# Layer 2's expert FFN in a fused four-layer kernel: features dealt out every eleventh, SiLU formed from tanh, and another order of units

## The chip, the cores and the metric

One core of a Trainium2 chip runs the whole program in one launch. The metric is device time in microseconds (us) from launch to end; lower is better. The engines that appear in the text: TensorE (PE in the profile; PEld is its weight loading, which overlaps it), VectorE (DVE), ScalarE (ACT), GpSimd (POOL) and SyncE (SP, which here only issues transfers). SBUF is the on-chip memory of 128 partitions, PSUM the memory that TensorE writes its results to.

## The reference

The reference is a gated network of four layers over x, 64 sequences of 64 tokens with 128 features (4096 tokens). Each layer adds a mixer and an FFN to x, each behind a layer norm and a scalar gate tanh(g):

```python
x = x + tanh(g_xattn[n]) * mixer_n(layernorm(x), ctx)
x = x + tanh(g_ffn[n]) * ffn_n(layernorm(x))          # n = 0..3, eight stages in all
```

The change is in layer 2's FFN, a mixture of 8 experts with 176 features each, of which every token uses the best two, plus one shared expert of 176 features:

```python
E, K, I = (8, 2, 176)
probs = jax.nn.softmax(x @ gate_w.T, axis=-1)
topk_w, topk_i = jax.lax.top_k(probs, K)
topk_w = topk_w / jnp.sum(topk_w, axis=-1, keepdims=True)
combine = jnp.sum(jax.nn.one_hot(topk_i, E) * topk_w[..., None], axis=1)
g = jnp.einsum('th,ehi->eti', x, w_gate)
u = jnp.einsum('th,ehi->eti', x, w_up)
eo = jnp.einsum('eti,eih->eth', jax.nn.silu(g) * u, w_down)
out = jnp.einsum('te,eth->th', combine, eo)
sg = jax.nn.sigmoid(x @ shared_gate_w.T)
out = out + sg * (jax.nn.silu(x @ sw_gate) * (x @ sw_up) @ sw_down)
```

The other stages that the text names: layer 0's FFN (a mixture with one expert chosen per head; lines 1236 and 1291 are its large products), layer 1's attention (lines 1349 to 1474), layer 1's FFN (an autoencoder picks an adapter per sequence; line 1585 gathers its rows), layers 2's and 3's attention (function `attend8`, lines 1637 to 1728), and layer 3's FFN, which quantises by the largest value over all tokens and therefore can't finish before every token has come through.

## The kernel before

**Units.** The 4096 tokens are eight groups of 512. A stage n applied to a group g is a unit, written "ng". The list `ORDER` (line 2135) names all 64 units in the order in which they are recorded; a group passes through its stages in turn, and groups overlap. The first unit of a stage also records the stage's constants, and the weights of a stage are loaded after the first unit of the stage before.

**The planner.** Nothing is issued as written. Every call on an engine is recorded as an operation with its inputs, outputs and an estimated duration (`cost`, line 221). `Plan.order` (line 401) then schedules all operations at once: at each step it picks, among the operations that are ready, the one that can start first, preferring earlier recorded ones, and so fixes the order of instructions on every engine and queue. On the chip every engine works through its fixed list in that order. Temporary tiles come from pools of slots (`SLOTS`, line 41: 45 slots of 2 KB per partition, `b2k`, and the 8 banks of PSUM, `ps`). `TABLES` (line 218) says which function of ScalarE needs which table; where an operation needs another table than the last one, the planner adds 1300 ns to it, and holds it back for up to 1000 ns in favour of others. `Tanh` is marked as needing no table of its own. Where the planner sees TensorE without work, `keep_clock` (line 482) puts in fillers: products of the identity with itself whose result nobody reads. They are recorded under line 2158.

**Layer 2's FFN (lines 1816 to 1926).** Per group of 512 tokens:

- `ln_T`: layer norm and transposition, so that xT has features on partitions and tokens along the row.
- `route` (1847): scores, softmax, best two experts and their weights, and the shared expert's sigmoid, which ends as cw, nine combine weights per token (gate factor included).
- `spread` (1885): cw is transposed (1889), copied (1891) and written to device memory as cwd, nine rows of 512 (1893).
- The nine experts' features lie side by side as 9 x 176 = 1584 columns. They are taken in 13 chunks: twelve of 128 columns and one of 48. A chunk has features on partitions. Since 176 is no multiple of 128, a chunk holds parts of one or two experts, and each chunk has its own tile cb, in which every partition holds its expert's combine weights for the 512 tokens. cb is filled from cwd by one or two transfers (1906), 20 per unit, 160 in all.
- Per chunk: two products on TensorE, pg (1914) and pu (1915); SiLU of pg on ScalarE (1917); times pu on VectorE (1918); times cb on GpSimd (1919); and the down product on TensorE, summed over the chunks in one bank (1920). For the chunk of 48, one product with both weights side by side (1911).
- At the end a copy (1922), a transposition back and an addition to x (1924).

The weights stand in SBUF for the whole run: gate and up weights as 128 x 1536, loaded in one transfer each (1824) on ScalarE's queue; the down weights as 13 chunks of 128 rows, loaded by 29 transfers (1833) on SyncE's queue.

Of the kernel before, what the change touches and what calls it, by code (L numbers as in the profile page):

```python
# [23 lines left out]
AF = mybir.ActivationFunctionType  # L24
ALU = mybir.AluOpType
AX = mybir.AxisListType

P = 128
# [5 lines left out]
GT = 512  # L34
# [730 lines left out]
def bc(ap, axis, n):  # L765

    ap = ap.unsqueeze(axis)
    shape = list(ap.shape)
    shape[axis] = n
    return ap.to_broadcast(shape)  # L770
# [8 lines left out]
def first_onehot(k, vals, best, rank, tag):  # L779

    nc = k.nc
    p, m, n = vals.shape
    eq = k.tile([p, m, n], tag=tag + "e")
    nc.vector.tensor_tensor(eq, vals, bc(best, 2, n), ALU.is_equal)
    nc.vector.tensor_tensor(eq, eq, bc(rank, 1, m), ALU.mult)
    top = k.tile([p, m], tag=tag + "t")
    nc.vector.tensor_reduce(top, eq, AX.X, ALU.max)
    oh = k.tile([p, m, n], tag=tag + "o")  # L790
    nc.vector.tensor_tensor(oh, eq, bc(top, 2, n), ALU.is_equal)
    return oh
# [42 lines left out]
def transpose4(k, src):  # L835

    ps = k.ps()
    k.plan.wait(src)
    for t in range(4):
        k.nc.tensor.transpose(ps[:, t * P : (t + 1) * P], src[:, t, :], k.ident)  # L840
    return ps


def ln_T(k, g):

    ps = transpose4(k, layernorm(k, g))
    xT = k.tile([P, GT], tag="xT")
    k.nc.scalar.copy(xT, ps)
    return xT
# [966 lines left out]
def l2_ffn_weights(k):  # L1816
    k.l2f = {"gate": k.load("l2f_gate")}

    last = k.l2f["last"] = k.fixed("w_l2f_last", [P, 112])
    k.nc.gpsimd.memset(last, 0.0)  # L1820
    at, end = k.done
    for n, name in enumerate(("wg", "wu")):
        t = k.l2f[name] = k.fixed("w_l2f_" + name, [P, 1536])
        k.nc.scalar.dma_start(out=t, in_=k.a["l2f_" + name][:, :1536])
        k.nc.scalar.dma_start(out=last[:, 64 * n : 64 * n + 48], in_=k.a["l2f_" + name][:, 1536:])
        k.plan.after = k.plan.ops[at + (end - at) * (n + 1) // 3]
    src = k.a["l2f_wd"]
    wd = k.l2f["wd"] = k.fixed("w_l2f_wd", [P, 13, P])
    for n in range(18):
        r = 88 * n  # L1830
        while r < 88 * n + 88:
            end = min(88 * n + 88, (r // P + 1) * P)
            k.nc.sync.dma_start(
                out=wd[r % P : r % P + end - r, r // P, :], in_=src[r - 88 * n : end - 88 * n, n * P : (n + 1) * P]
            )
            r = end


def l2_ffn(k):
    nc = k.nc  # L1840
    E, I, HID = 8, 176, 9 * 176
    CH = [(c, min(P, HID - c)) for c in range(0, HID, P)]
    W = k.l2f

    gate = k.tg[:, 1, 2:3]

    def route(xT, g):

        pr = k.ps()
        for t in range(TG):  # L1850
            nc.tensor.matmul(
                pr[:, t * (E + 1) : (t + 1) * (E + 1)], xT[:, t * P : (t + 1) * P], W["gate"], start=True, stop=True
            )
        lg = pr[:, : TG * (E + 1)].rearrange("p (t e) -> p t e", e=E + 1)
        pb = k.tile([P, TG, E], tag="pb")
        m = k.tile([P, 4, TG], tag="m")
        nc.vector.tensor_reduce(m[:, 0], lg[:, :, 0:E], AX.X, ALU.max)
        nc.vector.tensor_tensor(pb, lg[:, :, 0:E], bc(m[:, 0], 2, E), ALU.subtract)
        nc.scalar.activation(pb, pb, AF.Exp)
        nc.vector.tensor_reduce(m[:, 1], pb, AX.X, ALU.add)  # L1860
        nc.vector.reciprocal(m[:, 1], m[:, 1])
        nc.vector.tensor_tensor(pb, pb, bc(m[:, 1], 2, E), ALU.mult)
        nc.vector.tensor_reduce(m[:, 2], pb, AX.X, ALU.max)
        oh1 = first_onehot(k, pb, m[:, 2], k.rank8, tag="l2oh1")
        nc.vector.scalar_tensor_tensor(pb, oh1, -2.0, pb, ALU.mult, ALU.add)
        nc.vector.tensor_reduce(m[:, 3], pb, AX.X, ALU.max)
        oh2 = first_onehot(k, pb, m[:, 3], k.rank8, tag="l2oh2")

        nc.vector.tensor_tensor(m[:, 0], m[:, 2], m[:, 3], ALU.add)
        nc.vector.reciprocal(m[:, 0], m[:, 0])  # L1870
        nc.vector.scalar_tensor_tensor(m[:, 2], m[:, 2], gate, m[:, 0], ALU.mult, ALU.mult)
        nc.vector.scalar_tensor_tensor(m[:, 3], m[:, 3], gate, m[:, 0], ALU.mult, ALU.mult)
        cw = k.tile([P, TG, E + 1], tag="cw")
        nc.vector.tensor_tensor(oh1, oh1, bc(m[:, 2], 2, E), ALU.mult)
        nc.vector.tensor_tensor(oh2, oh2, bc(m[:, 3], 2, E), ALU.mult)
        nc.vector.tensor_tensor(cw[:, :, 0:E], oh1, oh2, ALU.add)

        sg = k.tile([P, TG], tag="sg1")
        nc.scalar.activation(sg, lg[:, :, E], AF.Exp, scale=-1.0)
        nc.vector.tensor_scalar(sg, sg, 1.0, None, ALU.add)  # L1880
        nc.vector.reciprocal(sg, sg)
        nc.vector.tensor_scalar(cw[:, :, E], sg, gate, None, ALU.mult)
        return cw

    def spread(cw):

        pc = k.ps()
        for t in range(TG):
            nc.tensor.transpose(pc[: E + 1, t * P : (t + 1) * P], cw[:, t, :], k.ident)
        cT = k.tile([E + 1, GT], tag="cwT")  # L1890
        nc.scalar.copy(cT, pc[: E + 1, :])
        d = k.dram([E + 1, GT], "cwd")
        nc.sync.dma_start(out=d, in_=cT)
        return d

    def unit(g):
        xT = ln_T(k, g)
        cwd = spread(route(xT, g))
        py = k.ps()
        for c, (c0, cn) in enumerate(CH):  # L1900
            cb = k.tile([P, GT], tag="cb")
            r = c0
            while r < c0 + cn:
                e = r // I
                end = min(c0 + cn, (e + 1) * I)
                nc.sync.dma_start(out=cb[r - c0 : end - c0, :], in_=cwd[e : e + 1, :].to_broadcast([end - r, GT]))
                r = end
            pg = k.ps()
            if cn < P:
                pu = pg[64 : 64 + cn]  # L1910
                nc.tensor.matmul(pg[: 64 + cn], W["last"], xT, start=True, stop=True)
            else:
                pu = k.ps()
                nc.tensor.matmul(pg, W["wg"][:, c0 : c0 + cn], xT, start=True, stop=True)  # L1914
                nc.tensor.matmul(pu, W["wu"][:, c0 : c0 + cn], xT, start=True, stop=True)  # L1915
            h = k.tile([P, GT], tag="h")
            nc.scalar.activation(h[:cn], pg[:cn], AF.Silu)  # L1917
            nc.vector.tensor_tensor(h[:cn], h[:cn], pu, ALU.mult)  # L1918
            nc.gpsimd.tensor_tensor(h[:cn], h[:cn], cb[:cn], ALU.mult)  # L1919
            nc.tensor.matmul(py, W["wd"][:cn, c, :], h[:cn], start=(c == 0), stop=(c == len(CH) - 1))  # L1920
        yT = k.tile([P, TG, P], tag="yT")
        nc.scalar.copy(yT.rearrange("p t i -> p (t i)"), py)
        xg = k.x[g].rearrange("p t d -> p (t d)")
        nc.vector.tensor_tensor(xg, xg, transpose4(k, yT), ALU.add)

    return unit
# [44 lines left out]
def l3_ffn(k):  # L1971
# [163 lines left out]
ORDER = [  # L2135
    (int(n), int(g))
    for n, g in (
        "02 00 03 01 06 04 10 05 11 20 07 21 30 31 40 12 41 50 13 51 16 22 14 60 15 61 23 70 26 32 17 24 "
        "71 42 25 33 36 27 43 34 46 52 35 44 62 45 37 53 56 47 63 54 66 55 64 65 72 57 67 73 76 74 75 77"
    ).split()  # L2140
]

# [1 line left out]
def program(tc, a):  # L2144
    with ExitStack() as es:
# [9 lines left out]
        for g in early:  # L2155
            nc.sync.dma_start(out=k.x[g], in_=xin[g])
        constants(k)
        plan.spare = (sys._getframe().f_lineno, k.ident, k.ident.t.writes[-1][0])
        mixers = (l0_xattn, l0_ffn, l1_xattn, l1_ffn, l2_xattn, l2_ffn, l3_xattn)
        weights = (None, l0_ffn_weights, l1_xattn_weights, l1_ffn_weights, l2_xattn_weights, l2_ffn_weights,  # L2160
                   l3_xattn_weights)
        layers = [None] * 8
# [123 lines left out]
```

## Time and profile before

| | us |
|---|---|
| median of 18 runs | 1902.12 |
| lowest and highest of them | 1893.21, 1907.34 |
| the profiled execution | 1899.2 |
| its span, first to last instruction | 1897.5 |
| mean granted TensorE clock in it | 0.973 |

| engine | busy us | share of the span | instructions |
|---|---|---|---|
| PE | 1812.7 | 96% | 16703 |
| PEld | 1066.6 | 56% | 16703 |
| DVE | 1361.0 | 72% | 3194 |
| ACT | 1106.5 | 58% | 2957 |
| POOL | 1024.1 | 54% | 1655 |

One fp32 product on TensorE appears in the profile as two instructions (two passes), each with a weight load; so 104 products are 208 rows. The ends of matrix products are modelled, so that a pass of 512 columns has a duration of 592 ns in the rows though the next may start earlier. In a row of the groups, the number after the bar is the group's busy time, then the mean duration of one in ns, then the time in which the engine stood idle just before members of the group, and what ended most of that. In the chain of waits, the work that ended last is followed back from the end, step by step, to what released it: PE has 70% of it, DVE 11%, POOL 8%, ACT 4%. 121.11 MB move by DMA in 122231 packets, a mean of 64 GB/s.

### The profile page before, as it was taken

To read this page: it belongs to the slowest core of one execution; us is meant where nothing else is said; L and a number is where in the kernel's file an instruction comes from. 1 tells how busy PE (TensorE), PEld (TensorE's weight loads), DVE (VectorE), ACT (ScalarE), POOL (GpSimd) and SP (SyncE) were. 2 spreads that over 40 slices of the span, in tenths; PEclk is the share of its full clock that TensorE was granted. 3 is DMA by queue.
4 is the path that set the end of the run, shared out by engine and by line. 5 is a ranking of instruction groups with operands and counts; after the bars stand their busy time and mean duration, and the time that the engine had idled before them with its cause. 6 is when DMAs were issued, how large, how long until landed. Compare 5 with 4: busy or idle time off the path is not lost.

```text
span 1897.5 us, 44773 instructions
## 1 busy us (share of the span) xinstructions
PE 1812.7 (96%) x16703; PEld 1066.6 (56%) x16703; DVE 1361.0 (72%) x3194; ACT 1106.5 (58%) x2957; POOL 1024.1 (54%) x1655
## 2 busy tenths in 40 slices
PE   7999999999999999999999999999899989999996
PEld 4555456655554445645465655675466555555675
DVE  6786887679858476667877578769458966855667
ACT  6664347745463345524368543887367766867655
POOL 7862446645433454303548354837477469476546
PEclk8899999999999999999999999999799989999999
DMA  6302230013325221031300021000141034153021
GB/s 191 113 22 82 57 101 20 2 39 115 98 76 147 60 72 46 15 103 36 95 21 13 20 65 59 24 2 3 38 115 33 29 97 120 30 141 101 32 74 45
DMA packets 122231, 121.11 MB, mean 64 GB/s; under 512 B 58378, under 2 KB 78485, under 8 KB 122013
## 3 DMA queue, kind: packets, MB, share of 16 engines
q1 hardware_dynamic: 112541, 102.66, 19.1%
q10 hardware_dynamic: 6400, 9.25, 1.6%
q0 software_dynamic: 3072, 6.33, 1.2%
q8 instruction: 132, 2.16, 0.5%
q14 instruction: 86, 0.70, 0.1%
HBM read 98.22 MB, written 8.18 MB: 56 GB/s over the span
## 4 chain that ended last, share of the span: by engine, by line
PE 70%; DVE 11%; POOL 8%; ACT 4%; issue 3%; DMA 3%; SPq 0%; another core or an unknown queue 0%; ACTq 0%; DVEq 0%; POOLq 0%
PE ps L1236 11%; PE ps L1291 8%; PE ps L840 8%; POOL b L776 5%; PE ps L1920 4%; PE ps L1914 4%; PE ps L1915 4%; PE ps L1470 3%; PE ps L1701 3%; PE ps L1349 3%; PE ps L1457 2%; PE ps L1560 2%; PE ps L1263 2%; PE ps L1663 2%; DVE b2k L1289 2%
## 5 line engine op out<-in xcount | busy, mean ns | idle before, releaser
L776 POOL TENSOR_TENSOR b<-b,neghalf 128x8 f32<-128x8 f32 (+1 forms) x208 | 303.3, 1458 | 17.0
L1291 PE MATMUL ps<-b2k,w_l0f_oe 128*128 128x512 f32 x512 | 233.2, 599 | 4.5 <-DMA b2k<-ohd 1.9
L1236 PE MATMUL ps<-w_l0f_ve,b2k 128*128 128x512 f32 x512 | 236.2, 602 | 0.5 <-DVE b4k L1105 0.2
L775 POOL TENSOR_SCALAR b<-b 128x8 f32<-128x8 f32 (+1 forms) x208 | 44.2, 213 | 320.4 <-DVE b L804 197.2
L1289 DVE TENSOR_TENSOR b2k<-b2k,b2k 128x512 f32<-128x512 f32 x256 | 174.2, 728 | 29.3 <-PE ps L1291 11.4
L1242 DVE COPY_PREDICATED b2k<-b1k,ps 128x512 f32<-128x512 int32 x224 | 161.8, 726 | 44.0 <-PE ps L1236 26.2
L1919 POOL TENSOR_TENSOR b2k<-b2k,b2k 128x512 f32<-128x512 f32 (+1 forms) x104 | 130.8, 1284 | 109.6 <-DMA b2k<-cwd 60.9
L1104 DVE TENSOR_REDUCE b<-ps 128x8 f32<-128x512 f32 x224 | 146.4, 681 | 52.0 <-PE ps L1674 14.8
L1291 PEld LDWEIGHTS ps<-b2k,w_l0f_oe 128*128 128x128 f32 x512 | 93.3, 190 | 121.2 <-issue 78.1
L1107 ACT ACTIVATE b4k<-b4k 128x64 f32<-128x64 f32 x512 | 125.8, 250 | 46.3 <-DVE b4k L1105 44.1
L1105 DVE TENSOR_TENSOR b4k<-ps,b 128x512 f32<-128x512 f32 x224 | 148.7, 678 | 4.0 <-PE ps L840 2.2
L1236 PEld LDWEIGHTS ps<-w_l0f_ve,b2k 128*128 128x128 f32 x512 | 93.5, 191 | 102.3 <-issue 84.1
L840 PE MATMUL ps<-ident,b2k 128*128 128x128 f32 x896 | 133.4, 277 | 9.1 <-ACT b2k L815 3.0
L840 PEld LDWEIGHTS ps<-ident,b2k 128*128 128x128 f32 x896 | 102.5, 141 | 67.2 <-issue 33.9
L840 PE MATMUL ps<-ident,b4k 128*128 128x128 f32 x896 | 127.3, 278 | 5.9 <-ACT b4k L1689 1.6
L840 PEld LDWEIGHTS ps<-ident,b4k 128*128 128x128 f32 x896 | 102.5, 142 | 50.4 <-issue 28.6
L1918 DVE TENSOR_TENSOR b2k<-b2k,ps 128x512 f32<-128x512 f32 (+1 forms) x104 | 70.0, 682 | 75.9 <-ACT b2k L1917 38.5
L1360 DVE TENSOR_TENSOR b2k<-ps,b 128x512 f32<-128x512 f32 x128 | 87.4, 686 | 30.4 <-POOL b L1357 18.4
L1689 ACT ACTIVATE b4k<-b4k 128x512 f32<-128x512 f32 x128 | 76.1, 630 | 51.0 <-DVE b4k L1105 45.0
L1354 DVE TENSOR_REDUCE b<-b2k 128x8 f32<-128x512 f32 x128 | 84.7, 677 | 27.6 <-ACT b2k L1351 24.8
L1920 PE MATMUL ps<-b2k,w_l2f_wd 128*128 128x512 f32 (+1 forms) x208 | 102.3, 610 | 2.0 <-POOL b2k L1919 1.9
L1440 POOL TENSOR_TENSOR b4k<-b4k,b 128x512 f32<-128x512 f32 x64 | 67.5, 1075 | 65.9 <-DVE b L1437 54.9
(368 smaller groups left out, 4091.3 us busy)
## 6 DMA issues: line engine op xcount, KB each, us to landing
b2k<-ohd SPq DMA_DIRECT2D x256, 128.0 KB
b2k<-cwd SPq DMA_DIRECT2D x40, 256.0 KB
b2k<-in_ctxT SPq DMA_DIRECT2D x32, 256.0 KB
b2k<-b2k SPq DMA_DIRECT2D x128, 64.0 KB
b2k<-b2k SPq DMA_DIRECT2D x32, 128.0 KB
b2k<-cwd SPq DMA_DIRECT2D x16, 224.0 KB
b2k<-cwd SPq DMA_DIRECT2D x16, 192.0 KB
b2k<-cwd SPq DMA_DIRECT2D x16, 160.0 KB
```

The source lines that it names most:

```text
L776: k.nc.gpsimd.tensor_tensor(out, out, k.neghalf[:, :n], ALU.pow)
L840: k.nc.tensor.transpose(ps[:, t * P : (t + 1) * P], src[:, t, :], k.ident)
L1104: nc.vector.tensor_reduce(mx, src, AX.X, ALU.max)
L1105: nc.vector.tensor_tensor(out, src, bc(mx, 2, S), ALU.subtract)
L1107: nc.scalar.activation(out[:, n, :], out[:, n, :], AF.Exp, accum_out=den[n])
L1236: nc.tensor.matmul(pe, xT[:, t * P : (t + 1) * P], W["ve"][:, e * 512 : (e + 1) * 512], start=True, stop=True)
L1242: nc.vector.copy_predicated(acc, bc(ohi[:, t * H : (t + 1) * H, e], 2, DH), pe.rearrange("p (h d) -> p h d", d=DH))
L1289: nc.vector.tensor_tensor(so, oT[c], pick[:, u, :], ALU.mult)
L1291: nc.tensor.matmul(py, W["oe"][:, n * P : (n + 1) * P], so, start=(n == 0), stop=(n == C * E - 1))
L1360: nc.vector.tensor_tensor(n.rearrange("p c (r d) -> p (c r) d", r=2), ps.rearrange("p (h d) -> p h d", d=DH), bc(r, 2, DH), ALU.mult)
L1919: nc.gpsimd.tensor_tensor(h[:cn], h[:cn], cb[:cn], ALU.mult)
L1920: nc.tensor.matmul(py, W["wd"][:cn, c, :], h[:cn], start=(c == 0), stop=(c == len(CH) - 1))
```

## The change

1. **Features every eleventh.** The 8 x 176 = 1408 features of the eight experts are 128 x 11. Chunk c (0 to 10) now holds on partition q the feature 11 q + c, read from the weights with a step of 11 columns. The expert of that feature is (11 q + c) // 176 = q // 16 for every c. So one tile cbe holds the combine weights for all eleven chunks, and one tile cbs, with the shared expert's weight on every partition, serves the two chunks of the shared expert (128 and 48 features, as columns 1408 to 1583). Two transfers per unit fill them. The down weights are loaded so that their rows follow the same order, by 16 transfers of 8 x 11 rows and three for the shared expert.
2. **SiLU from tanh.** silu(g) = g (1 + tanh(g / 2)) / 2. ScalarE computes t = tanh(pg / 2); VectorE computes w = pg times cb and then h = (t + 1) times pu; GpSimd multiplies h by w. The factor 1/2 goes into the combine weights when they are copied after their transposition (1890 of the changed kernel).
3. **Order of units.** The list ORDER has the same 64 units in another order; the first group that enters layer 1's attention, whose keys are prepared early, is group 1 where it was group 0.

Line numbers inside `l2_ffn` move by -1 or by a few lines: 1911, 1912 and 1908 are the changed kernel's products for gate, up and the last chunk, 1915 the tanh, 1917 and 1918 VectorE's products, 1919 GpSimd's, 1920 the down product.

```diff
@@ l2_ffn_weights
     for n, name in enumerate(("wg", "wu")):
-        t = k.l2f[name] = k.fixed("w_l2f_" + name, [P, 1536])
+        t = k.fixed("w_l2f_" + name, [P, 1536])
         k.nc.scalar.dma_start(out=t, in_=k.a["l2f_" + name][:, :1536])
+        k.l2f[name] = [t[:, c:1408:11] for c in range(11)] + [t[:, 1408:]]
...
-    for n in range(18):
-        r = 88 * n
-        while r < 88 * n + 88:
-            end = min(88 * n + 88, (r // P + 1) * P)
-            k.nc.sync.dma_start(
-                out=wd[r % P : r % P + end - r, r // P, :], in_=src[r - 88 * n : end - 88 * n, n * P : (n + 1) * P]
-            )
-            r = end
+    for n in range(16):
+        k.nc.sync.dma_start(
+            out=wd[8 * n : 8 * n + 8, 0:11, :], in_=src[:, n * P : (n + 1) * P].rearrange("(q c) d -> q c d", c=11)
+        )
+    for p0, c, n, r0, rows in ((0, 11, 16, 0, 88), (88, 11, 17, 0, 40), (0, 12, 17, 40, 48)):
+        k.nc.sync.dma_start(out=wd[p0 : p0 + rows, c, :], in_=src[r0 : r0 + rows, n * P : (n + 1) * P])
@@ l2_ffn, spread
-        nc.scalar.copy(cT, pc[: E + 1, :])
+        nc.scalar.activation(cT, pc[: E + 1, :], AF.Copy, scale=0.5)
@@ l2_ffn, unit
         cwd = spread(route(xT, g))
+        cbe = k.tile([P, GT], tag="cbe")
+        nc.sync.dma_start(out=cbe, in_=cwd[0:E, :].unsqueeze(1).to_broadcast([E, 16, GT]))
+        cbs = k.tile([P, GT], tag="cbs")
+        nc.sync.dma_start(out=cbs, in_=cwd[E : E + 1, :].to_broadcast([P, GT]))
         py = k.ps()
         for c, (c0, cn) in enumerate(CH):
-            cb = k.tile([P, GT], tag="cb")
-            r = c0
-            while r < c0 + cn:
-                e = r // I
-                end = min(c0 + cn, (e + 1) * I)
-                nc.sync.dma_start(out=cb[r - c0 : end - c0, :], in_=cwd[e : e + 1, :].to_broadcast([end - r, GT]))
-                r = end
+            cb = cbe if c < 11 else cbs
...
-                nc.tensor.matmul(pg, W["wg"][:, c0 : c0 + cn], xT, start=True, stop=True)
-                nc.tensor.matmul(pu, W["wu"][:, c0 : c0 + cn], xT, start=True, stop=True)
+                nc.tensor.matmul(pg, W["wg"][c], xT, start=True, stop=True)
+                nc.tensor.matmul(pu, W["wu"][c], xT, start=True, stop=True)
             h = k.tile([P, GT], tag="h")
-            nc.scalar.activation(h[:cn], pg[:cn], AF.Silu)
-            nc.vector.tensor_tensor(h[:cn], h[:cn], pu, ALU.mult)
-            nc.gpsimd.tensor_tensor(h[:cn], h[:cn], cb[:cn], ALU.mult)
+            nc.scalar.activation(h[:cn], pg[:cn], AF.Tanh, scale=0.5)
+            w = k.tile([P, GT], tag="hw")
+            nc.vector.tensor_tensor(w[:cn], pg[:cn], cb[:cn], ALU.mult)
+            nc.vector.scalar_tensor_tensor(h[:cn], h[:cn], 1.0, pu, ALU.add, ALU.mult)
+            nc.gpsimd.tensor_tensor(h[:cn], h[:cn], w[:cn], ALU.mult)
@@ ORDER
-        "02 00 03 01 06 04 10 05 11 20 07 21 30 31 40 12 41 50 13 51 16 22 14 60 15 61 23 70 26 32 17 24 "
-        "71 42 25 33 36 27 43 34 46 52 35 44 62 45 37 53 56 47 63 54 66 55 64 65 72 57 67 73 76 74 75 77"
+        "01 03 02 00 11 04 10 21 05 20 31 13 06 12 30 41 07 14 40 51 15 23 22 50 61 16 24 60 33 32 71 17 "
+        "25 43 42 70 34 26 44 35 53 52 27 45 36 54 46 37 55 63 62 47 56 64 57 65 66 73 72 67 74 75 76 77"
```

## The prediction

> **What bounds the kernel now.** I read the page's slices first, then the groups of instructions, the stretches, TensorE's own waits, and timelines around single instructions. The slices show busy tenths in 40 equal parts of the span.
>
> ```profile
> PE   7999999999999999999999999999899989999996
> DVE  6786887679858476667877578769458966855667
> ACT  6664347745463345524368543887367766867655
> ```
>
> TensorE (PE) is at nine tenths nearly everywhere; the others have room. A busy PE is not a PE at its peak, so I looked for proof: in the chain of waits 54 passes of L1291 follow each other in 23.18 us, 0.43 us for a 512-column pass, and wherever layer 2's FFN runs its passes also start 0.43 us apart. PE is the bound, and a change elsewhere pays only through PE's gaps: visible idle time, and the fillers (L2158) that the planner puts where it sees a gap. The groups (line, engine, operation, tiles, count, busy us, mean ns, idle before):
>
> ```profile
> L1917 ACT ACT_TABLE_LOAD x41 | 52.6, 1283 | 1.8 <-PE ps L1701 0.9 <-PE ps L1914 0.3
> L1689 ACT ACT_TABLE_LOAD x31 | 39.8, 1283 | 2.9 <-DVE b4k L1105 2.4
> L1918 DVE TENSOR_TENSOR b2k<-b2k,ps 128x512 f32<-128x512 f32 x96 | 64.5, 682 | 72.1 <-ACT b2k L1917 35.0 <-PE ps L1915 29.7 <-ACT b2k L1114 6.5
> L1563 DVE SCALAR_TENSOR_TENSOR b2k<-ps,w_l1f_bd,b2k 128x512 f32<-128x512 f32 x64 | 43.3, 743 | 7.4 <-PE ps L1560 7.4
> L2158 PE MATMUL ps<-ident 128*128 128x128 f32 x494 | 66.7, 286 | 1.4 <-POOL ident L859 1.4
> ```
>
> The reader sees 72 table loads between SiLU and Exp, the price of an instruction of the kind added on VectorE (743 ns), and 66.7 us of fillers. Six of the eight FFN units of layer 2 run between 1350 and 1800 us. The stretches (length; busy us of PE, PEld, DVE, ACT, POOL; clock):
>
> ```profile
> 1350.00:1800.00 450.00, 435.02 (x3942) 263.06 (x3941) 311.23 (x885) 315.63 (x574) 281.69 (x530) 0.97 0.27 74
> ...
> 1450.00:1500.00 50.00, 49.05 (x365) 26.53 (x362) 45.40 (x108) 36.61 (x68) 22.20 (x49) 1.00 0.12 35
> ```
>
> PE idles 450 - 435.0 = 15.0 us there. What ended that idle time (us in total, times, longest):
>
> ```profile
> PE ps L1604 <- DVE b4k L1105: 2.9, 1, 2.9
> PE ps L1920 <- POOL b2k L1919: 1.9, 2, 1.3
> ...
> PE ps L840 <- DVE b2k L1918: 1.6, 1, 1.6
> ...
> PE ps L840 <- ACT b4k L1689: 1.1, 2, 0.7
> PE ps L1701 <- ACT b2k L1693: 0.9, 2, 0.7
> ```
>
> So the edited lines and the ScalarE lines beside them hold PE up for only 1.9 + 1.6 + 1.1 + 0.9 = 5.5 us.
>
> **The change, part by part.**
>
> *Fillers and order.* The built programs' instruction lists hold the same 9350 matrix products and transposes on PE in both kernels; only their order and the fillers differ, 247 before and 214 after. Up to the first L0 units there are 46 against 51; from there on 201 against 163. The missing ones are those that stood between layer 2's and layer 3's units (15 and some 30); the chain at the end, where the quantisation needs a maximum over all tokens, keeps its fillers. One costs 66.7 / 247 = 0.270 us, so 33 fewer are -8.9 us. Bounds: 0, if the planner's gaps merely open again as waits, and -8.9. I take -8.9, because the one list is closed over exactly the stretches in which the other had holes.
>
> *SiLU to tanh.* ScalarE's Activate stays one per chunk (104, about 598 ns, L1917). The lists hold 94 table loads before and 14 after: 80 x 1.283 = 102.6 us of ScalarE work go. ScalarE is 70% busy in the late stretch (315.6 of 450), so most of this is off the path; what PE has waited for it is the 1.1 + 0.9 us above, and through L1918, which stood 35.0 us behind L1917, another 1.6, all within the 5.5. Around one switch (start, us, instruction):
>
> ```profile
> 1378.22 0.60 ACT L1917 ACTIVATE b2k<-ps 128x512 f32<-128x512 f32 x1
> 1378.84 1.28 ACT L1107 ACT_TABLE_LOAD   x1
> 1380.13 0.26 ACT L1107 ACTIVATE b4k<-b4k 128x64 f32<-128x64 f32 x1
> ```
>
> The load begins 0.02 us after one Activate and ends 0.01 us ahead of the next. The Trainium skill ("ScalarE: Activation LUTs", What ACT_TABLE_LOAD costs) adds a drain of about 1.38 us, 2.66 us per switch, which would free an estimated 213 us; this trace shows no such drain. As PE's waits behind ScalarE are measured by themselves, the sum stays the same by either.
>
> *The products.* VectorE did one product per chunk (682 ns) and now does two: the gate times the combine weight, again PSUM with SBUF (682 ns), and (tanh + 1) times up, of L1563's kind: 104 x 0.743 = +77.3 us on VectorE. GpSimd's product stays (104 x about 1284 ns, L1919). In the late stretch, 78 of the 104 chunks of before, VectorE goes from 311.2 to 369.2 of 450 us, 82%. What hides it: PE's own queue, as at 1450 to 1500 us, where VectorE is 91% busy (45.4 of 50) and PE still 98%. Without that cover each chunk would cost 0.743 us. I take 0; bounds 0 and +23 us (third rival below). From matrix product to h nothing gets longer but 0.06 us: the new product runs beside tanh.
>
> *Combine weights.* A unit used to fetch 13 spread tiles by 20 transfers (160 issues, 24.8 MB in all); now two of 256 KB serve all chunks (16 issues, 4.0 MB). With the down weights (29 to 19 issues) SyncE sheds 154 issues, at L1906's median of 0.382 us some 59 us of queue time. The chain of waits has four pieces waiting for these transfers, 6.34 + 3.81 and 5.01 + 4.95 us, yet PE is busy 15.7 of 17 and 15.4 of 16 us around them. The gain is within the 1.9 us of L1920 behind L1919 plus the idle time that the trace names otherwise; I take the 1.9, which is part of the 5.5 already.
>
> *Stationary operands with a step.* The gate and up weights of eleven chunks are read with a step of 11 elements: 88 chunks x 2 matrices x 2 passes = 352 loads. No row shows such a load. Two loads now (PEld, start and us):
>
> ```profile
> 1579.41 0.19 PEld L1914 LDWEIGHTS ps<-b2k,w_l2f_wg 128*128 128x128 f32 x1 [0.24 <-issue]
> 1579.84 0.19 PEld L1914 LDWEIGHTS ps<-b2k,w_l2f_wg 128*128 128x128 f32 x1 [0.24 <-issue]
> ```
>
> They take 0.19 us and the loading side rests 0.24 us before the next, under a 0.43 us pass; 32 loads of L1470 run back to back in 3.65 us, 0.114 us each. A load may thus grow to more than three times its rate and stay hidden; the longest among L1914's, 0.337 us, would still fit. I take 0 (both bounds by rows). The Trainium skill speaks against this edit: "SBUF — State Buffer" (Door 1: The DMA port swizzle) says that memory is read in 16-byte lines and that each access to a new line pays, so that four fp32 are the free stride. Halving the rate (an estimate, as the page gives no factor) makes 0.23 us per load, hidden under a 0.43 us pass, and exposed by about 0.12 us only where a chunk's first load follows a short pass: 88 x 0.12, some 10 us, which would make the sum 1895.
>
> *Sum.* The profiled execution took 1899.2 us (span 1897.5 and 1.7 around it). 1899.2 - 8.9 - 5.5 + 0 + 0 = 1884.8. The median of the runs, 1902.1, lies 2.9 above it, so I predict 1887.7, rounded to 1888.
>
> **The rivals.**
>
> *A larger gain.* All 15.0 us of idle time in the late stretch go instead of 5.5, and with them the clock's loss there (0.97 over 450 us, 13.5 us): 1888 - 9.5 - 13.5 = 1865. For it: the transfers and 102.6 us of ScalarE work vanish from just this stretch. Against it: the idle time is spread over many causes, and the lowest clock (0.78 at 1325 to 1350 us, 0.67 in the 25 us after) comes with sixteen gathers of L1585 in a row, which the change keeps.
>
> *No change.* The missing fillers reopen as waits and a late VectorE takes back the 5.5: 1902. For it: PE was 96.7% busy in the stretch already.
>
> *Slower: the wait for the combine weights moves to VectorE.* GpSimd stood 60.9 us for them; the instruction that reads them now is VectorE's product, on an in-order engine behind which stand the evictions (L1104, L1105, L1242, L1360) that free PSUM for PE. How long the transfer takes (SP issues the write and the first spread, POOL's product starts):
>
> ```profile
> 1651.77 0.29 SPq L1893 DMA_DIRECT2D cwd<-b2k  x1
> 1653.28 11.70 SPq L1906 DMA_DIRECT2D b2k<-cwd  x20
> 1657.48 1.27 POOL L1919 TENSOR_TENSOR b2k<-b2k,b2k 128x512 f32<-128x512 f32 x1 [17.38 <-DMA b2k<-cwd]
> ```
>
> 4.2 us from issue to use, eight times. If at each unit VectorE stands long enough to hold PE as long as its worst wait for VectorE above, 2.9 us, the price is 8 x 2.9 = 23.2 us: 1899.2 - 8.9 + 23.2 + 2.9 = 1916. It decides from 14.4 / 8 = 1.8 us of PE time per unit. For it: VectorE's load rises too. Against it: 2 transfers share the rings where 20 did, and the planner places the product after the transfer.
>
> *The step is dear.* If a stepped load outlasts the pass, every 0.1 us above 0.43 costs 352 x 0.1 = 35 us: 1923 or more. It needs loads nearly four times as slow.
>
> **How the numbers follow.** Runs of this kernel differ by some 0.2%, so 0.2% (3.8 us) is about what a measurement can tell. Chances: forecast 0.50 (its own range 1874 to 1898), larger gain 0.15, no change 0.10, slower 0.25 (VectorE 0.18, the step 0.07). Faster is 0.50 + 0.15 = 0.65, same 0.10, slower 0.25. The range reaches down to the larger gain, 1864, and up to 1912, near the VectorE rival, leaving out the step and the worst of VectorE.
>
> **What would show it.** Right: some 14 table loads; the L1914 and L1915 successors' passes still 0.43 us apart with their loads below 0.4 us; DVE busy near 1438 us (1361.0 + 77.3); PE's idle time in the late stretch under 12 us; fillers near 58 us (214 x 0.270). Wrong: PE's idle time put down to VectorE lines that stand behind a wait for the cwd transfers; loads longer than 0.43 us; or more PE idle time in the middle of the span, where the new order, not the FFN, would be the cause.

## The result, and the profile after

The changed kernel takes 1983.35 us (median of 10 runs, 1975.24 to 1990.51); the kernel before, run beside it, 1900.39 us (62 runs, 1892.95 to 1911.75). The ratio is 1.0438, with a 95% interval of 1.0419 to 1.0457: slower by some 83 us, where 1888 us and a gain had been forecast, and outside the range of 1864 to 1912.

The profiled execution has a span of 1992.4 us. The slices of its page (40 equal parts, busy tenths; PEclk is the clock granted to TensorE):

```profile
PE   8999999999989999999999899989899998999996
DVE  5778877767868667765777677958557866777667
ACT  5553457533353342774338444857337542544555
PEclk8799999999999899999999899989899986989998
```

PE is still at nine tenths, but less evenly than before, and ScalarE and VectorE have not become full: no other engine took the bound over. The totals say where the 94.9 us of longer span (1992.4 - 1897.5) lie: PE is busy 1874.2 us (before 1812.7) with 66 passes fewer, so 61.5 us go to slower passes, and it idles 118.2 us (before 84.8). The mean granted clock fell from 0.973 to 0.949. By these two figures TensorE lost 101.6 us of its span to the clock where it had lost 51.2, some 50 us more: an estimate that would account for most of the 61.5. The groups that answer to those shown of before, and the new product:

```profile
L1918 DVE SCALAR_TENSOR_TENSOR b2k<-b2k,ps 128x512 f32<-128x512 f32 (+1 forms) x104 | 70.8, 683 | 47.5 <-PE ps L1912 43.0 <-ACT b2k L1745 1.4 <-ACT b2k L1915 1.3
L1917 DVE TENSOR_TENSOR b2k<-ps,b2k 128x512 f32<-128x512 f32 (+1 forms) x104 | 67.8, 681 | 53.5 <-ACT b2k L1915 46.1 <-DMA b2k<-cwd 5.7 <-POOL b2k L1919 1.6
L2158 PE MATMUL ps<-ident 128*128 128x128 f32 x428 | 61.6, 297 | 1.9 <-POOL ident L859 1.4 <-DVE b1k L1091 0.5
L1911 PEld LDWEIGHTS ps<-b2k,w_l2f_wg 128*128 128x128 f32 x192 | 57.5, 317 | 28.1 <-issue 9.1 <-DVE b2k L1918 3.2 <-DVE b2k L1917 3.1
```

The reader sees the two VectorE products at 0.68 us each, the fillers at 61.6 us, weight loads of 317 ns (before 193), and only 5.7 us in which VectorE itself stood for the combine weights. The late stretch (length; busy us and count of PE, PEld, DVE, ACT, POOL; clock; DMA share; GB/s):

```profile
1350.00:1800.00 450.00, 417.74 (x3480) 267.30 (x3480) 310.53 (x798) 222.30 (x532) 270.30 (x452) 0.91 0.09 28
```

PE idles 32.3 us there (15.0 before), the clock is 0.91 instead of 0.97, and fewer passes get through. PE's longest waits (us in all, times, longest) are not on the FFN's edited lines:

```profile
PE ps L1663 <- DVE b4k L1105: 11.4, 7, 4.4
...
PE ps L1618 <- ACT b1k L1612: 5.3, 2, 4.1
...
PE ps L840 <- ACT b4k L1689: 4.5, 4, 2.1
PE ps L840 <- ACT b2k L1693: 4.4, 7, 1.0
```

They are waits of the attention of layers 2 and 3 for its own softmax and evictions, and of layer 1's FFN (L1618). None of these views names the cause. One reading points to it: how long the bank that a gate product (pg) was written to waits for its last reader. The sixth unit of layer 2's FFN in order of time, from the timeline of the changed kernel (start, us, engine, line):

```profile
1631.47 1.21 PE L1911 MATMUL ps<-b2k,w_l2f_wg 128*128 128x512 f32 x1
...
1633.63 0.60 ACT L1915 ACTIVATE b2k<-ps 128x512 f32<-128x512 f32 x1 [1.29 <-PE ps L1911]
...
1655.04 0.22 DVE L1881 TENSOR_SCALAR b<-b,tgates 128x4 f32<-128x4 f32 x1
...
1676.36 0.38 PE L1888 MATMUL ps<-ident,b 128*9 128x128 f32 x1
...
1679.59 0.64 SPq L1899 DMA_DIRECT2D b2k<-cwd  x1
...
1684.84 0.68 DVE L1917 TENSOR_TENSOR b2k<-ps,b2k 128x512 f32<-128x512 f32 x1
```

tanh has read pg after 2.2 us, but the product w = pg x cb needs the combine weights, whose transfer is issued 48 us after the gate pass. Until 1684.84, 53.4 us after the first gate pass, the bank can't be given back, and by then seven chunks' gate passes have started, each into a bank of its own. PSUM has eight. The same reading for all units of layer 2's FFN, from the first gate pass to the start of the first instruction that is the bank's last reader (before: SiLU; after: the product w), and how many chunks' gate passes have started by then; beside it when the first product with combine weights runs:

| unit, in order of time | before: bank read after, us | before: weights used after, us | after: bank read after, us | after: gate passes started |
|---|---|---|---|---|
| 1 | 1.5 | 20.0 | 62.8 | 6 |
| 2 | 2.4 | 24.7 | 22.2 | 6 |
| 3 | 2.2 | 54.9 | 58.3 | 6 |
| 4 | 2.5 | 67.4 | 17.3 | 7 |
| 5 | 2.6 | 66.0 | 31.4 | 7 |
| 6 | 1.7 | 42.1 | 53.4 | 7 |
| 7 | 3.2 | 32.1 | 52.3 | 7 |
| 8 | 2.6 | 19.4 | 19.4 | 5 |
| sum | 18.7 | | 317.1 | |

Before, the combine weights were just as late, 19 to 67 us after the first gate pass. That is not the work of routing itself: VectorE's instructions on the lines of `route` take 33.8 us in all eight units together; the rest is mostly waiting between them. But what waited for the weights was h in SBUF, of which there are 45 slots. Now it is pg in PSUM.

In the unit shown, the finished weights (L1881, done at 1655.26) wait 21.1 us for their transposition (L1888), which needs a bank of PSUM itself. The same gap is 31.7 and 35.7 us in units 1 and 7 and at most 17.3 us in the kernel before. So held banks may also put off the weights that would free them; no run tests this link by itself.

### The profile page after: what moved, and what is told of

It is laid out like the page before. It is cut to its first block, busy times and chain, and to the rows that moved or that the text cites. A ratio compares the mean times of both kernels' runs of the same rounds, so it can differ in the third digit from the quotient of the medians.

```text
span 1992.4 us, 44228 instructions
## 1 busy us (share of the span) xinstructions
PE 1874.2 (94%) x16637; PEld 1138.4 (57%) x16637; DVE 1426.8 (72%) x3298; ACT 1009.1 (51%) x2877; POOL 1033.8 (52%) x1655
## 4 chain that ended last, share of the span: by engine, by line
PE 73%; DVE 10%; POOL 6%; ACT 4%; DMA 3%; issue 3%; SPq 0%; another core or an unknown queue 0%; ACTq 0%; DVEq 0%; POOLq 0%
PE ps L1236 11%; PE ps L1291 10%; PE ps L840 8%; PE ps L1911 5%; PE ps L1920 5%; PE ps L1912 4%; POOL b L776 4%; PE ps L1701 3%; PE ps L1470 3%; PE ps L1349 2%; PE ps L1386 2%; PE ps L1663 2%; PE ps L1457 2%; PE ps L1263 2%; DVE b L1104 1%
## 5 line engine op out<-in xcount | busy, mean ns | idle before, releaser
L776 POOL TENSOR_TENSOR b<-b,neghalf 128x8 f32<-128x8 f32 (+1 forms) x208 | 303.4, 1459 | 17.3
L1236 PE MATMUL ps<-w_l0f_ve,b2k 128*128 128x512 f32 x512 | 242.3, 613 | 3.8 <-issue 3.1
L1291 PE MATMUL ps<-b2k,w_l0f_oe 128*128 128x512 f32 x512 | 228.1, 597 | 2.6 <-DVE b2k L1289 2.3
L1919 POOL TENSOR_TENSOR b2k<-b2k,b2k 128x512 f32<-128x512 f32 (+1 forms) x104 | 129.9, 1275 | 74.2 <-DVE b2k L1917 41.9
L840 PE MATMUL ps<-ident,b4k 128*128 128x128 f32 x896 | 144.7, 301 | 14.3 <-ACT b4k L1689 4.5
L1107 ACT ACTIVATE b4k<-b4k 128x64 f32<-128x64 f32 x512 | 125.1, 250 | 52.5 <-DVE b4k L1105 52.3
L1915 ACT ACTIVATE b2k<-ps 128x512 f32<-128x512 f32 (+1 forms) x104 | 61.8, 596 | 175.3 <-PE ps L1911 140.9
L840 PEld LDWEIGHTS ps<-ident,b4k 128*128 128x128 f32 x896 | 112.9, 154 | 59.9 <-issue 27.7
L1911 PE MATMUL ps<-b2k,w_l2f_wg 128*128 128x512 f32 x192 | 109.1, 651 | 3.1 <-DVE b2k L1918 1.8
L1912 PE MATMUL ps<-b2k,w_l2f_wu 128*128 128x512 f32 x192 | 105.9, 634 | 3.9 <-DVE b2k L1917 1.9
```

The source lines that it names most:

```text
L776: k.nc.gpsimd.tensor_tensor(out, out, k.neghalf[:, :n], ALU.pow)
L1107: nc.scalar.activation(out[:, n, :], out[:, n, :], AF.Exp, accum_out=den[n])
L1236: nc.tensor.matmul(pe, xT[:, t * P : (t + 1) * P], W["ve"][:, e * 512 : (e + 1) * 512], start=True, stop=True)
L1291: nc.tensor.matmul(py, W["oe"][:, n * P : (n + 1) * P], so, start=(n == 0), stop=(n == C * E - 1))
L1911: nc.tensor.matmul(pg, W["wg"][c], xT, start=True, stop=True)
L1912: nc.tensor.matmul(pu, W["wu"][c], xT, start=True, stop=True)
```

## The experiments

Ratios are to the kernel before on the same chip in the same job; one chip ran it at 1861 us, another at 1899. Theories at the start: the *step* (slower weight loads), the *products* (VectorE's added work), the *order* of units.

**The step, twice.** The changed kernel with contiguous chunks, and the kernel before with a step of 11; both have their instructions in the same order as the kernel they come from.

The host lays the columns out to suit.

```
after_contig
-        k.l2f[name] = [t[:, c:1408:11] for c in range(11)] + [t[:, 1408:]]
+        k.l2f[name] = [t[:, P * c : P * c + P] for c in range(12)]
before_step11
-        t = k.l2f[name] = k.fixed("w_l2f_" + name, [P, 1536])
+        t = k.fixed("w_l2f_" + name, [P, 1536]); k.l2f[name] = [t[:, c:1408:11] for c in range(11)] + [t[:, 1408:]]
...
-                nc.tensor.matmul(pg, W["wg"][:, c0 : c0 + cn], xT, start=True, stop=True)
+                nc.tensor.matmul(pg, W["wg"][c], xT, start=True, stop=True)
```

> The changed kernel, same instructions in the same order, but the host lays the gate and up weights out so that each chunk's 128 columns are contiguous and no weight load has a step. Step theory (a load with a step of 11 takes 0.32 us instead of 0.19, which starves TensorE): the loads of L1911 and L1912 are back at 0.19 us and the time at 1885 to 1905 us. Products theory (the second VectorE product in the path from matrix product to h): 1970 to 1990 us, since it is still there. Order theory (the new order of units does worse on the chip): 1970 to 1990 us.

> The kernel before, same instructions in the same order; only the gate and up weights lie in memory so that eleven chunks are read with a step of 11 elements, as in the changed kernel. Step theory: the loads of L1914 and L1915 grow from 0.19 to 0.32 us and the time to 1950 to 1990 us. If longer loads stay hidden under the 0.43 us passes, as predicted, and the products or the order are the cause: loads 0.32 us, time 1895 to 1905 us.

Measured: 1981.09 us, ratio 1.044 (1.040 to 1.048), no different from the changed kernel; and 1907.05 us, ratio 1.0016 (0.9989 to 1.0044). In the groups of the kernel before with the step:

```profile
L1914 PE MATMUL ps<-b2k,w_l2f_wg 128*128 128x512 f32 x192 | 103.7, 622 | 0.6 <-issue 0.6
...
L1914 PEld LDWEIGHTS ps<-b2k,w_l2f_wg 128*128 128x128 f32 x192 | 58.0, 315 | 21.0 <-issue 6.2 <-DVE b L804 0.4 <-ACT b2k L1448 0.2
```

A load takes 315 ns instead of 193 and stays hidden: PE idles 0.6 us ahead of these passes. The step theory falls.

**The order, on old and new operations.** Each kernel with the other's `ORDER`, nothing else; after_old_order is the same exchange the other way round.

```
before_new_order
-        "02 00 03 01 06 04 10 05 11 20 07 21 30 31 40 12 41 50 13 51 16 22 14 60 15 61 23 70 26 32 17 24 "
-        "71 42 25 33 36 27 43 34 46 52 35 44 62 45 37 53 56 47 63 54 66 55 64 65 72 57 67 73 76 74 75 77"
+        "01 03 02 00 11 04 10 21 05 20 31 13 06 12 30 41 07 14 40 51 15 23 22 50 61 16 24 60 33 32 71 17 "
+        "25 43 42 70 34 26 44 35 53 52 27 45 36 54 46 37 55 63 62 47 56 64 57 65 66 73 72 67 74 75 76 77"
```

> The kernel before with the new order of units and nothing else. Step theory and products theory: 1890 to 1915 us, as the operations of layer 2's FFN are the old ones. Order theory: 1960 to 1990 us, with about 200 us of TensorE time at half clock.

> The changed kernel with the order of units of the kernel before. Step theory: 1960 to 1990 us, the loads of L1911 and L1912 still at 0.32 us. Products theory: 1960 to 1990 us. Order theory: 1885 to 1905 us, and TensorE's stretches at half clock back from about 204 us to about 103 us in total.

Measured: 1957.21 us, 1.031 (1.0263 to 1.0356), and 2018.45 us, 1.062 (1.0583 to 1.0656). The order theory comes within 3 us of its range in the first and loses the second: with the old order the changed operations are worse still. The other two theories miss both. The time at half clock, estimated from the mean granted clocks of 0.962 and 0.950 (the clock in these traces is either full or half), is some 150 and 200 us, where the order theory had asked for 200 and 103. So there is a cost of the operations (6.2% under the old order, 1.2% under the new one beside the old operations) and one of the order, and they don't add up.

**The operations in an unchanged list.** The planner works with the old operations; only while it writes the instructions out are they replaced or doubled. Every engine keeps its order.

```
before_tanh_same_list, where each operation is written out
+    if op.line == 1917:
+        args[2], kw["scale"] = AF.Tanh, 0.5
before_tanh_product_same_list, besides
+    if op.line == 1918:
+        h, _, pu, _ = args
+        call(nc.vector.scalar_tensor_tensor, [h, pu, 0.0, h, ALU.mult, ALU.add], {})
```

> The kernel before with every engine's instructions in exactly its own order; only the function of layer 2's 104 activations is tanh in place of SiLU when the instruction is written out, so that 82 table loads of ScalarE go. It leaves out the sigmoid factor of SiLU. List theory (what costs is the rewritten order of instructions on the engines, not the operations): 1885 to 1900 us, a few microseconds under before. Operations theory (tanh, products and freed ScalarE themselves upset the pipeline): 1930 us or more. My own step for the table loads in the prediction would give some 5 us less than before.

> As the kernel with tanh in before's own list, and at each of the 104 chunks one more VectorE product that reads PSUM (h = 0 x up + h, then the old product), of about 0.74 us, in series ahead of the old one: 77 us more on VectorE and a longer way to h than in the changed kernel. It leaves out the sigmoid factor of SiLU. List theory: 1885 to 1910 us. Products theory: 1950 to 1980 us.

Measured: 0.9969 (0.9949 to 0.9990), and 1.0187 (1.0127 to 1.0248). Tanh's page:

```profile
PE 1789.2 (97%) x16703; PEld 1057.9 (57%) x16703; DVE 1361.8 (74%) x3194; ACT 1003.3 (54%) x2875; POOL 1024.8 (55%) x1655
```

ScalarE does 103.2 us less than before (1106.5) with 82 instructions fewer, and the kernel gains 0.31% (0.10 to 0.51), 5.8 us of 1861. The added product costs 1.0187 - 0.9969 = 2.2%, some 41 us for 71.1 us of VectorE work (104 at 684 ns). For the added product both theories missed: the list theory said at most 1910 of the 1899 us of that time (1.006), the products theory at least 1.027.

**The product taken out of the changed kernel's list.**

```
after_without_product, where each operation is written out
+    if op.line == 1917:
+        CB[op.args[0].t] = args[2]
+        return
+    if op.line == 1919:
+        args[2] = CB.pop(op.args[2].t)
```

> The changed kernel with every engine's instructions in its own order, but without the 104 added VectorE products of the gate (L1917), 71 us of VectorE; GpSimd multiplies with the combine weights instead. It leaves out the factor of the gate. List theory: 1965 to 1990 us, as the list is that of the changed kernel. Products theory: 1890 to 1920 us.

Measured: 1947.2 us where before takes 1861.18, ratio 1.0457 (1.0428 to 1.0486). The changed kernel did not run in this job; beside its 1.0438 from another chip, nothing is gained. tanh is now the gate bank's last reader, 1.3 to 2.2 us after the first pass in every unit, and yet unit 6's stretch looks as it did. First the changed kernel, from first gate pass to first product:

```profile
1631.50:1684.40 52.90, 44.80 (x275) 28.06 (x276) 32.18 (x94) 19.40 (x42) 9.47 (x19) 0.63 0.06 17
```

then the same stretch of the list without the product:

```profile
1579.20:1631.00 51.80, 43.71 (x273) 27.88 (x274) 31.69 (x92) 19.45 (x41) 8.82 (x19) 0.63 0.05 13
```

and the sixth unit of the kernel before, from its first gate pass to that of its last full chunk:

```profile
1615.40:1654.40 39.00, 38.18 (x406) 23.46 (x406) 32.36 (x95) 32.29 (x58) 15.63 (x47) 1.00 0.01 3
```

PE is 84 to 85% busy at a clock of 0.63 with the product and without it; before it was 98% at 1.00. As far as ratios of two chips can tell, the loss is therefore in the *list*: the product costs through the list that was planned with it, not through its run.

**How touchy a list is.** Two neighbouring late units exchanged, nothing else.

```
-        "71 42 25 33 36 27 43 34 46 52 35 44 62 45 37 53 56 47 63 54 66 55 64 65 72 57 67 73 76 74 75 77"
+        "71 42 25 33 36 27 43 34 46 52 35 44 62 45 37 53 56 63 47 54 66 55 64 65 72 57 67 73 76 74 75 77"
```

> The kernel before with two neighbouring units of the order exchanged (47 and 63, late in the kernel) and nothing else; the planner then rewrites the list from about there on. If the list of before is an unusually good one, so that most rewritings cost: 1910 to 1960 us, with more TensorE idle time and half-clock time after 1400 us. If lists hardly matter and the two orders compared so far are special: 1895 to 1905 us.

Measured: 1888.0 us beside 1861.18, ratio 1.0136 (1.0092 to 1.018). The size is in the expected band, the mechanism is not: in the late stretch PE is 435.9 us busy at a clock of 0.99, against 435.0 and 0.97; the list holds 138 passes more (16841 against 16703), all of them fillers. The two other lists tried on the old operations thus cost 1.4 and 3.1%, with no bank held and no operation added.

**The bank theory.** The table above gave a new theory: w = pg x cb can't run before the combine weights are there, `Plan.order` gives a bank back only when its last reader is in the list, and so it writes a list for a machine whose banks fill up, until one to three are left, for 17 to 63 us, eight times. Two edits test it from both sides. One keeps all added work and lets go of the bank; the other adds no work to the kernel before and holds a bank.

```
after_gate_first
-            w = k.tile([P, GT], tag="hw")
-            nc.vector.tensor_tensor(w[:cn], pg[:cn], cb[:cn], ALU.mult)
-            nc.vector.scalar_tensor_tensor(h[:cn], h[:cn], 1.0, pu, ALU.add, ALU.mult)
-            nc.gpsimd.tensor_tensor(h[:cn], h[:cn], w[:cn], ALU.mult)
+            nc.vector.scalar_tensor_tensor(h[:cn], h[:cn], 1.0, pg[:cn], ALU.add, ALU.mult)
+            nc.vector.tensor_tensor(h[:cn], h[:cn], pu, ALU.mult)
+            nc.gpsimd.tensor_tensor(h[:cn], h[:cn], cb[:cn], ALU.mult)
before_up_held
-            nc.vector.tensor_tensor(h[:cn], h[:cn], pu, ALU.mult)
-            nc.gpsimd.tensor_tensor(h[:cn], h[:cn], cb[:cn], ALU.mult)
+            w = k.tile([P, GT], tag="hw")
+            nc.vector.tensor_tensor(w[:cn], pu, cb[:cn], ALU.mult)
+            nc.gpsimd.tensor_tensor(h[:cn], h[:cn], w[:cn], ALU.mult)
```

> The changed kernel with its order of units, transfers, tanh and two VectorE products per chunk of the same kinds, but their operands are exchanged: first (tanh + 1) x gate, then x up, and GpSimd multiplies with the combine weight. So no VectorE product that reads a PSUM bank waits for the combine weights; the way to h is one product longer. Bank theory (in the changed kernel the gate's PSUM bank is held until the combine weights have come back, 17 to 63 us at the start of each of the eight units): first bank read within 4 us of the first gate pass in every unit, and the time between 0.99 and 1.015 of before. VectorE-load theory (104 more products on VectorE): 1.03 to 1.05, as the load is the same and the chain is longer. Order theory (the new order of units): 1.03 to 1.05.

> The kernel before, with SiLU, its old order of units and its 104 VectorE products and 104 GpSimd products of the same shapes; only who multiplies what is exchanged: VectorE multiplies up (in PSUM) with the combine weight, and GpSimd multiplies that with SiLU's result. VectorE's work is unchanged, no operation is added; a PSUM bank now waits for the combine weights. Bank theory: 1.03 to 1.07 of before, and several up passes of each unit ahead of the first read of their banks. VectorE-load theory, step theory and order theory: 0.995 to 1.01.

Measured: 1924.83 us, 1.0129 (1.0099 to 1.0159), and 2001.64 us, 1.054 (1.0498 to 1.0582). Exchanging two operands in the old kernel costs more than the whole change did. Its timeline around the fourth unit (the transfer is the first of the unit's 20):

```profile
1497.25 0.59 PE L1915 MATMUL ps<-b2k,w_l2f_wu 128*128 128x512 f32 x1
...
1555.48 0.33 SPq L1906 DMA_DIRECT2D b2k<-cwd  x1
...
1559.78 0.68 DVE L1919 TENSOR_TENSOR b2k<-ps,b2k 128x512 f32<-128x512 f32 x1
```

The up bank is held for 62.5 us; over the eight units it is 290.7 us (16 to 70 us), with the up passes of five to eight chunks started each time. With the gate first, the sixth unit reads:

```profile
1594.67 0.81 PE L1911 MATMUL ps<-b2k,w_l2f_wg 128*128 128x512 f32 x1
...
1597.01 0.68 DVE L1916 SCALAR_TENSOR_TENSOR b2k<-b2k,ps 128x512 f32<-128x512 f32 x1
```

The bank is read 1.9 to 2.8 us after the first gate pass in every unit; after that the combine weights may be as late as they like. The late stretch, first with the bank let go, then with the up bank held:

```profile
1350.00:1800.00 450.00, 428.61 (x3748) 287.56 (x3748) 345.11 (x890) 235.55 (x547) 289.06 (x495) 0.98 0.11 32
```

```profile
1350.00:1800.00 450.00, 409.24 (x3174) 245.95 (x3171) 261.86 (x744) 250.41 (x464) 236.69 (x433) 0.86 0.23 62
```

The clock is 0.98 with the bank let go against 0.86 with it held, with 0.97 before and 0.91 after the change; but the bank isn't all, as the old operations under the new order, with no bank held, stand at 0.93 there. Over the whole span VectorE has the larger load in the faster of the two, 1429.7 us against 1366.7, which the products theory can't explain.

A list can be good or bad by chance, so the lists have to be seen together. The three that were planned with a bank held for the combine weights (the changed kernel, after_old_order, before_up_held) stand at 1.044 to 1.062. Those planned without one stand at 1 to 1.031, and lower under the fitted orders below. That the bank costs is shown by this and by the two edits. How much of the changed kernel's own 4.4% is the bank's is not: its list stands 3.1% above that of after_gate_first and 1.2% above that of before_new_order, all three with the same order of units.

**What is left.** The changed order, features and transfers, with SiLU and the old products (the factor 1/2 in the combine weights goes too); then the kernel with the gate first, its chunks contiguous, under an order fitted to it; and the kernel before under an order fitted to it. "Fitted" means that units were moved until the planner's own plan ended earlier.

```
after_with_silu
-            nc.scalar.activation(h[:cn], pg[:cn], AF.Tanh, scale=0.5)
-            w = k.tile([P, GT], tag="hw")
-            nc.vector.tensor_tensor(w[:cn], pg[:cn], cb[:cn], ALU.mult)
-            nc.vector.scalar_tensor_tensor(h[:cn], h[:cn], 1.0, pu, ALU.add, ALU.mult)
-            nc.gpsimd.tensor_tensor(h[:cn], h[:cn], w[:cn], ALU.mult)
+            nc.scalar.activation(h[:cn], pg[:cn], AF.Silu)
+            nc.vector.tensor_tensor(h[:cn], h[:cn], pu, ALU.mult)
+            nc.gpsimd.tensor_tensor(h[:cn], h[:cn], cb[:cn], ALU.mult)
gate_first_fitted, besides the edits of after_gate_first and after_contig
+        "01 03 02 00 11 10 21 04 05 06 31 20 13 07 12 30 41 14 40 51 15 23 22 50 61 16 24 60 33 32 71 43 "
+        "17 25 42 70 34 26 44 35 53 52 27 45 36 54 46 37 55 63 47 56 62 64 72 57 66 65 73 67 75 76 77 74"
before_fitted
+        "02 00 03 01 06 04 10 05 11 20 07 21 30 31 40 12 41 50 13 51 22 16 60 14 15 70 61 23 26 32 17 24 "
+        "71 42 25 33 36 27 43 34 46 52 35 44 62 45 53 63 37 47 54 56 57 66 55 67 64 72 65 74 75 76 73 77"
```

> The changed kernel's order of units, its features with a step of 11 and its two combine-weight transfers per unit, with SiLU and the old products (one on VectorE, one on GpSimd). It tells what the parts of the change other than tanh and the products do together. Bank theory: 0.99 to 1.01 of before, as no PSUM bank waits for the combine weights. Order theory: 1.03 to 1.05, since the new order of units cost 1.031 on the kernel before.

> The kernel with the gate product first (which stood 1.013 over before), with the chunks' weights contiguous and with an order of units fitted to it, found by moving units until the planner's own plan ended earlier. If the 1.3% that are left after the banks are freed come from lists that the order of units makes: 0.985 to 1.000 of before. If they come from the operations (one more VectorE product, two combine-weight transfers): 1.008 to 1.02.

> The kernel before with an order of units fitted to it in the same way, nothing else. It tells how much the order alone is worth on the old operations, so that the run beside it can be read. If fitting carries over to the chip: 0.985 to 0.997 of before; if before's order is already the best that the chip knows: 1.000 to 1.015.

Measured: 1924.40 us, 1.0148 (1.0113 to 1.0183), between the two expectations; 1852.58 us, 0.9957 (0.9936 to 0.9977); and 1834.75 us, 0.9856 (0.9830 to 0.9882). So the 1.3% that the freed bank leaves is no fixed price of the operations: under a fitted order the version with tanh lies 0.4% below the kernel before. But the old operations gain more from fitting, and are then the fastest of that job: 0.9957 / 0.9856 = 1.010 between them. Whether this last per cent is the added product or only two orders fitted unequally well is open.

## Why the prediction was wrong, point by point

- **PE as the bound.** Right, and it stayed so (94% busy, 73% of the chain of waits). What I drew from it was not: that a change elsewhere can pay only through PE's gaps says nothing on how much it can cost.
- **Fillers, -8.9 us.** 33 fell away as counted, and their time went from 66.7 to 61.6 us, -5.1. But the step rested on the words "only their order and the fillers differ", with 0 as the worse bound. The order is no small thing: the new order of units alone costs the old operations 3.1% (58 us where -8.9 had been set), two units exchanged 1.4%. The bound on the costly side was missing; this is the first of the two steps that failed.
- **SiLU to tanh, -5.5 us.** Right in mechanism and size: 5.8 us (1.9 to 9.5) in an unchanged list, the table loads 98 before and 18 after. That the numbers are so close is partly luck: 1.9 of the 5.5 were the wait for the combine weights' product, which that run keeps, so 3.6 were tanh's. The rule of the Trainium skill ("ScalarE: Activation LUTs", What ACT_TABLE_LOAD costs) of a drain of about 1.38 us beside each load is not seen here: 82 loads at 1.283 us make 105 us, ScalarE's busy time fell by 103.2, and in the rows of the prediction the load starts 0.02 us after one Activate and ends 0.01 us ahead of the next.
- **The products, 0 us.** This is the second step that failed, and the one particular to this change. I wrote: "From matrix product to h nothing gets longer but 0.06 us: the new product runs beside tanh." That looks at the way to h from the moment all operands are there, and not at what each operand holds while it waits. GpSimd's product had always waited 19 to 67 us for the combine weights, with h in an SBUF slot; the new product takes that wait over with pg in a PSUM bank. Let go of the bank and 1.0438 becomes 1.0129, some 59 of the 83 us; hold a bank in the old kernel and it goes to 1.054. Beside the old operations under the same new order the cost is 1.2%, some 24 us, so its size stays open between the two. VectorE's added work was sized well (1426.8 - 1361.0 = 65.8 us, 77.3 foreseen). That it costs 0 when run is borne out where it runs beside tanh (after_without_product gains nothing without it); put in series into the old list, it costs 41 us, beyond my bound of 23.
- **The rival of the combine weights.** It named the right wait, at 0.18, and the wrong thing that is held. I priced VectorE's queue: eight times 2.9 us, from 4.2 us "from issue to use". VectorE stood 5.7 us in all. What decides is the time from the gate pass to the use, four to fifteen times as long, and the unit is banks, not queue time. All of it stood in the trace of before, in the starts of L1914 and L1919.
- **Combine weights in two transfers, 1.9 us.** 16 issues as foreseen, 22 MB less; no gain can be told: with SiLU kept, the new order stands at 1.0148 with these transfers and the step and at 1.031 without them, but the lists differ too.
- **The step, 0 us.** Right: 0.317 us a load, inside the bounds and under the pass, 1.0016. The halved rate that I took from "SBUF — State Buffer" (Door 1: The DMA port swizzle), an estimate of 0.23 us, was too mild; the load grew by two thirds, and not even the 10 us weighed there can be seen.
- **What would show it.** Loads below 0.4 us, VectorE near 1438 us (1426.8) and fillers near 58 us (61.6) came as set down; PE's idle time in the late stretch, set at under 12 us, came out at 32.3. The sign against the order came too: from 500 to 1350 us PE idles 39.8 us where it idled 27.0. So the signs said that the forecast had failed, but none asked how long a bank is held.

One rule of the Trainium skill bears on this: "Perfetto Trace Analysis" (Optimizing Tensor Performance, Matmuls) asks that independent products rotate through the banks, so that the eviction of one overlaps the next. In this case's rows the first bank is read 1.5 to 3.2 us after its pass before and its last reader starts 17 to 63 us after it in the changed kernel, the slower one.

## What to carry to other kernels

When a product is moved so that it reads PSUM, ask for each of its operands when it arrives, and pair a bank only with what is as early as the bank; late operands belong to the last product, out of SBUF. Read the hold of a bank from the trace (first write to last reader's start) before costing the instruction: 0.68 us of work held a bank for up to 63 us here. And where a planner writes the order, test operations in a fixed list and lists with fixed operations separately, and fit the order again before judging a change.

## What the runs showed that I had not expected

A list can keep a cost after its reason is gone: without the product, nothing held the banks any longer, and the stretch took 51.8 us instead of 52.9 at the same clock of 0.63. The clock falls without PE being idle for long: in that stretch PE is 85% busy, with 68 passes of L1663, on 32 x 64 of the array, and 128 of L1701, 18 columns wide, beside 27 gate and up passes; the kernel before had 44 gate and up passes in the 39 us of its sixth unit, with 96 and 192 of the others, at a clock of 1.00. Why the clock fell is left open. And the same kernel runs at 1861 us on one chip and at 1899 us on another, so times are compared only as ratios to the kernel before in the same job.
